# Gather buffers, edge weights and slot tiles in a four-layer graph network: which buffers a gather waits for

## The chip, the cores and the metric

The kernel runs on one core of one Trainium2 chip. The metric is the device time of one execution in microseconds. Three executions took 8439.02, 8420.99 and 8424.09 us, so the median is 8424.09 us. The profiled execution is a separate one and took longer than these; its numbers stand below.

## The reference

The input is a graph with 12,500 nodes of 128 features and 212,500 edges that are sorted by destination. Four layers follow each other; each one normalizes the node rows, gathers the row of every edge's source node, and adds a message into the row of the edge's destination node. Cut to what matters:

```python
h = relu(layernorm(x))                       # ahead of every layer
# layer 0: attention with 4 heads of 32
Wh = (h @ W.T).reshape(N, 4, 32)
attn = leaky_relu((concat([Wh[src], Wh[dst]], -1) * a).sum(-1), 0.2) + edge_attr_16 @ W_e.T
alpha = segment_softmax(attn, dst)
x = x + layernorm(gelu(segment_sum(alpha[..., None] * Wh[src], dst)))
# layer 1: weighted sum
x = x + gelu(gelu(segment_sum(h[src] * edge_weight1, dst)) @ W.T + b)
# layer 2: tensor product of h[src] with 9 edge features, a 32x32 mix for each path, sum over dst
x = x + segment_sum(tensor_product(h[src], edge_attr_9), dst)
# layer 3: mean over the neighbours, then a batch norm over the nodes
mean = segment_sum(h[src], dst) / maximum(segment_sum(1, dst), 1)
x = x + batchnorm(mean @ W_l.T + b_l + h @ W_r.T)
```

## The kernel before

**Tiles.** An edge group is 1024 edges, 8 slots of 128 (T = 8); there are NG = 208 groups. Because edges are sorted, the destinations of one group fall into a window of 128 nodes, so the sum over destinations is a matrix product of the 128 gathered rows with a one-hot matrix (`oh`), added up over the 8 slots in PSUM and then added into the accumulator `acc` (128 features by nodes) at the window's start.

**Gathers.** Each of the 8 slots of a group is one indirect DMA, issued from the POOL queue (`gather`, L621 to L624): 128 indices, 128 rows. Layers 0, 1 and 2 gather all 208 groups, that is 1664 gathers each. The 8 gathers of a group fill one tile `X`, and the pool of such tiles has a fixed depth: `bufs=LAG + 3`, which is 10, in layer 0 (L778), 4 in layer 1 (L1083), 4 in layer 2 (L1102), 3 in layer 3 (L1317). A gather of group g waits until the readers of the group that held the tile before are done. Gathers share eight completion semaphores, so each one waits also for the gather eight before it to have landed.

**Order.** In the edge loops the order on each engine is written out by hand (`manual_schedule`): per iteration of g, layer 1 gathers group g, builds its one-hot on DVE (L1085), adds group g-2 into `acc` (L1088) and multiplies group g-1 on PE (L1093). Layer 2 runs, per iteration, the ACT scaling A of group g (L1123), the mixer product of group g+1 (L1110 to L1113), the one-hot (L629), the add of group g-3 (L1158), the DVE products of group g (L1130 to L1142), the PE products of group g-1 (L1148) with their copy `R` on ACT (L1150, L1151), and the product `po` of group g-2 (L1155). Layer 0 trails its gathers by LAG = 7 groups, because the softmax weights of a group (`weights`, L800 to L846) are worked out four groups at a time; `spread_out` (L848) multiplies messages (L855, L860) and counts the edges of each node with a second product (L862), which DVE adds into `cnt` (L867).

**Between layers.** The first gather of a layer waits for all rows of the table that the node stage of the layer before stores (`htab`, `tab3`), so POOL idles there.

**Layer 3.** Only the first G0 = 138 groups, whose destinations lie in the first 64 blocks of 128 nodes (W0_ = 64), go through gathers. The sources of the other 34 windows (NW) are sorted in layer 1 (`Slots`, L905 to L1065) into slot tiles, 26 for each window, 884 in all. A slot tile (`tabled`, L1189 to L1287) takes four products `px` from a table in SBUF (L1256), a copy to `xb` on ACT (L1267) and one product `pw` (L1240); before each run of seven tiles, `fetch` and `prepare` load and build their one-hots (L1245, L1246). In the loop (L1314 to L1357), from g = 10 to 137, the tiles due in an iteration run first (L1336 to L1342) and then the eight products of group g-1 (L1348). One step of a node chunk (`node3`, four blocks of 128 nodes, 25 chunks) follows in each iteration, one chunk at a time (L1355 to L1357); a chunk has eight steps and divides by the counts: a load of `cnt16` (L521), a product that spreads it (L524), a maximum (L527), a reciprocal (L528) and a multiplication (L530). At the end `closing` applies the batch norm.

**Edge weights.** `eww` (L195, 6.5 KB in each partition) is loaded at the start (L307) and stays to the end. Layer 1 uses it, and so does a general path (from L1364) that runs only for graphs the windows don't fit.

Of the kernel before, what the change touches and what calls it, by code (L numbers as in the profile page):

```python
# [24 lines left out]
P = 128  # L25
T = 8
# [64 lines left out]
def gnn_kernel(ctx: ExitStack, tc, x, src, dst, ef16, ef9, ew, W0, We0, a0, lns, lnb, W1, b1,  # L91
# [18 lines left out]
    OT = OV // 4  # L110
    assert NS % P == 0
# [83 lines left out]
    eww = cst.tile([P, NG, T], F, name="eww")  # L195
# [3 lines left out]
    rough = cst.tile([P, 1], I, name="rough")  # L199
    begin = cst.tile([P, NW], I, name="begin")  # L200
# [9 lines left out]
    with tc.tile_pool(name="ed", bufs=1) as ep:  # L210
# [42 lines left out]
        vec.tensor_scalar(bi3, base, float(W0_ * P + 2 * W), None, op0=ALU.min)  # L253
# [37 lines left out]
        vec.scalar_tensor_tensor(worst, many, float(W), worst, op0=ALU.mult, op1=ALU.max)  # L291
        vec.tensor_scalar(many, red[:, 0, G0 - GM - 1 : G0 - GM], W0_ * P - 0.5, None, op0=ALU.is_gt)
# [14 lines left out]
    load_edges(eww, ew.rearrange("e o -> (e o)"), 0, NG, 0.0, 1)  # L307
# [98 lines left out]
    cnt16 = dram.tile([1, AW], B16, name="cnt16")  # L406
# [40 lines left out]
    def node0(sp, pp, k):  # L447
        b0, nb = k * NBK, min(NBK, NB - k * NBK)
        xv = sp.tile([P, nb, D], F, name="xv")
        load_rows(xv, x, b0, nb)  # L450
        pa = pp.tile([P, nb, P], F, name="pa")
        for j in range(nb):
            pe.transpose(pa[:, j, :], acc[:, (b0 + j) * P : (b0 + j + 1) * P], ident)
        yield
        vec.memset(acc[:, cols(k)], 0.0)
        o = sp.tile([P, nb, D], F, name="o")
        act.activation(o, pa, AF.Gelu)
        yield
        for n in norm(sp, o, nb, None):
            if n is None:  # L460
                yield
            else:
                o = n
        vec.tensor_tensor(o, o, lns_b[:, None, :].to_broadcast([P, nb, D]), ALU.mult)
        vec.tensor_tensor(o, o, lnb_b[:, None, :].to_broadcast([P, nb, D]), ALU.add)
        vec.tensor_tensor(xv, xv, o, ALU.add)
        yield from keep(sp, 0, k, xv)
# [48 lines left out]
    def node3(sp, pp, k, tabS, stats):  # L516

        b0, nb = k * NBK, min(NBK, NB - k * NBK)
        n = min(NBK * P, N - b0 * P)
        cn = sp.tile([1, nb * P], B16, name="cn")  # L520
        nc.sync.dma_start(cn, cnt16[:, cols(k)])  # L521
        yield
        pc = pp.tile([P, nb * P], F, name="pct")
        pe.matmul(pc, ones16, cn, start=True, stop=True)  # L524
        yield
        am = sp.tile([P, nb * P], F, name="am")
        vec.tensor_scalar(am, pc, 1.0, None, op0=ALU.max)  # L527
        vec.reciprocal(am, am)  # L528
        yield
        vec.tensor_tensor(am, acc[:, cols(k)], am, ALU.mult)  # L530
        pt = pp.tile([P, nb, P], F, name="pct")
        for j in range(nb):
            for i in range(3):
                pe.matmul(pt[:, j, :], tabS[:, b0 + j, i * P : (i + 1) * P], ident16, start=i == 0, stop=i == 2)
        yield
        hT = sp.tile([P, nb * P], F, name="hT")
        act.copy(hT, pt.rearrange("p j n -> p (j n)"))
        yield
        po = pp.tile([P, nb * P], F, name="pn")
        pe.matmul(po, WlT, am, start=True, stop=False)  # L540
        pe.matmul(po, WrT, hT, start=False, stop=True)  # L541
        yield
        act.activation(acc[:, cols(k)], po, AF.Identity, bias=bl_c)
        yield
        vec.bn_stats(stats[:, k, :], acc[:, b0 * P : b0 * P + n])
# [79 lines left out]

    def one_hot(sp, r, wgt=None, dt=F):
        s = sp.tile([P, T, W], dt, name="oh")
        if wgt is None:
            vec.tensor_tensor(s, iop[:, None, :].to_broadcast([P, T, W]), r[:, :, None].to_broadcast([P, T, W]),  # L629
                              ALU.is_equal)  # L630
        else:
            for t in range(T):
                vec.tensor_scalar(s[:, t, :], io, r[:, t : t + 1], wgt[:, t : t + 1], op0=ALU.is_equal, op1=ALU.mult)  # L633
        return s

    class Window:
# [7 lines left out]
        def load(self, b):  # L644
            ins, vals = nc.values_load_multi_w_load_instructions(b, engines=(self.engine,), min_val=0, max_val=AW - W)
            if len(self.ends) >= 2 and not self.ordered:
                for i in ins:
                    tc.add_manual_dep(i.ins, self.ends[-2].ins.name, NOSYNC, reason="registers")
            return vals[0]
# [4 lines left out]
    def sweep(xp, stream, window):  # L654
# [83 lines left out]

    H1 = H + 1
    vec.memset(acc, 0.0)  # L740
    with (tc.tile_pool(name="e0", bufs=2) as sp, tc.tile_pool(name="e0p", bufs=2, space=PSUM) as pp,
# [18 lines left out]
        cnt = sp.tile([1, AW], B16, name="cnt", bufs=1)  # L760
# [14 lines left out]
        def logits(g):  # L775

            e, rb, sdw = loads.pop(g)
            X = xs[g] = sp.tile([P, T, P + H], F, name="X", bufs=LAG + 3)  # L778
# [21 lines left out]
        def weights(i):  # L800
# [3 lines left out]
            d = sp.tile([P, L + 1], I, name="d")  # L804
            nc.sync.dma_start(d[:n], windows(dpad, c - HALO - 1, n, K, L + 1))
            lt = sp.tile([P, L, H], F, name="lt")
# [41 lines left out]
        def spread_out(g):  # L848

            X, ev = xs.pop(g), alphas.pop(g)  # L850
            S = sp.tile([P, T, W], F, name="oh")
            vec.tensor_tensor(S, iop[:, None, :].to_broadcast([P, T, W]),
                              rel[:, g, :, None].to_broadcast([P, T, W]), ALU.is_equal)
            msg = sp.tile([P, T, P], F, name="msg")
            vec.tensor_tensor(msg.rearrange("p t (h d) -> p t h d", h=H),  # L855
                              X[:, :, :P].rearrange("p t (h d) -> p t h d", h=H),
                              ev[:, :, :, None].to_broadcast([P, T, H, HD]), ALU.mult)
            pag = sums[g] = pp.tile([P, 2, W], F, name="pag", bufs=1)
            for t in range(T):
                pe.matmul(pag[:, 0, :], msg[:, t, :], S[:, t, :], start=t == 0, stop=t == T - 1)  # L860
            for t in range(T):
                pe.matmul(pag[:1, 1, :], ones[:, :1], S[:, t, :], start=t == 0, stop=t == T - 1)  # L862

        def add_up(g):
            win = ds(areg.load(bi[0:1, g : g + 1]), W)
            p = sums.pop(g)
            vec.tensor_tensor(cnt[:, win], cnt[:, win], p[:1, 1, :], ALU.add)  # L867
# [199 lines left out]
    kept = ctx.enter_context(tc.tile_pool(name="kept", bufs=1))  # L1067
    relc = kept.tile([P, NW, NT], F, name="relc")
    oversrc = kept.tile([SL, NW], I, name="oversrc")


    with (tc.tile_pool(name="e1", bufs=3) as sp, tc.tile_pool(name="e1p", bufs=2, space=PSUM) as pp,
# [6 lines left out]
        with tc.manual_schedule():  # L1079
            g = -1  # L1080
            while nodes.step(g := g + 1) or g < NG + 2:
                if g < NG:
                    X[g] = sp.tile([P, T, P], F, name="X", bufs=4)  # L1083
                    gather(X[g], htab[0], si[:, g, :])
# [4 lines left out]
                if 0 <= g - 1 < NG:  # L1089
                    p = pags[g - 1] = pp.tile([P, W], F, name="pag")  # L1090
                    s, r = S.pop(g - 1), X.pop(g - 1)
                    for t in range(T):
                        pe.matmul(p, r[:, t, :], s[:, t, :], start=t == 0, stop=t == T - 1)  # L1093
                slots.step(1 + g % 2)
            slots.close()


    def layer2(sp, pp):
        feats = feature_stream(ef9f, 9, 4, "ef", sp)

        def rows2(idx):
            X = sp.tile([P, T, P], F, name="X", bufs=4)  # L1102
# [59 lines left out]
    with (tc.tile_pool(name="e2", bufs=3) as sp, tc.tile_pool(name="e2p", bufs=2, space=PSUM) as pp,  # L1162
          tc.tile_pool(name="n2", bufs=2) as ns, tc.tile_pool(name="n2p", bufs=1, space=PSUM) as np_):
        rows2, mix, _, window2 = layer2(sp, pp)
# [24 lines left out]
    def tabled(sp, pp, xb, tabS, pm, stats, make):  # L1189
# [23 lines left out]
        def last(i):  # L1213

            xo = sp.tile([P, 3 * P], B16, name="xo")
            pool.indirect_dma_start(out=xo[:SL, :], out_offset=None, in_=tab3[:, :],
# [3 lines left out]
        def finish(i, pw):  # L1220
            s = sp.tile([P, P], F, name="s3", bufs=1)
            vec.tensor_reduce(s, pw.rearrange("p (k f) -> p f k", k=3), AX.X, ALU.add)
# [19 lines left out]
        for i in range(NW):  # L1242
            pw = None
            for jp in range(0, NT, PT):
                fetch(k + 2)  # L1245
                prepare(k + 1)  # L1246
                a, b = ready.pop(k)
                for jj in range(pieces[k][2]):
# [9 lines left out]
                    if j == OT:  # L1258
                        x = xo
                        act.copy(x[SL : 2 * SL, :], px[SL : 2 * SL, :])  # L1260
                        act.copy(x[2 * SL :, :], px[2 * SL :, :])
                        if i + 1 < NW:
                            xo = last(i + 1)
                    else:
                        x = xb[n_x % len(xb)]
                        n_x += 1
                        act.copy(x, px)  # L1267
                    if len(pend) == 2:
                        scatter()
                    if pw is None:  # L1270
                        while pend and pend[0][3]:
                            scatter()
                        pw = pp.tile([P, 3 * P], F, name="pw", bufs=1)
                    pend.append((x, b[:, jj, :], pw, j))
                    ends = [e for e in ends if next(e, "end") != "end"]
# [13 lines left out]
    with tc.tile_pool(name="l3", bufs=1) as lp:  # L1289
        stats = lp.tile([P, NK, 6], F, name="stats")  # L1290
        with (tc.tile_pool(name="t3", bufs=1) as tp, tc.tile_pool(name="e3", bufs=2) as sp,
# [3 lines left out]
            xb = [tp.tile([P, 3 * P], B16, name=f"xb{i}") for i in range(4)]  # L1295
# [7 lines left out]
            with tc.manual_schedule():  # L1303
# [10 lines left out]
                while g < G0 + 8 or alive or going or waiting:  # L1314
                    g += 1
                    if g < G0:
                        X[g] = sp.tile([P, T, 3 * P], B16, name="X", bufs=3)  # L1317
                        gather(X[g], tab3, si[:, g, :])
# [17 lines left out]
                    if alive and g >= first:  # L1336
                        goal = total if g >= last_ else total * (g - first + 1) // (last_ - first + 1)
                        while alive and (count < goal or goal == total):
                            alive = next(windows3, "end") != "end"
                            count += 1  # L1340
                            if g >= last_ and count % 8 == 0:
                                break  # L1342
                    h = g - 1
                    if 0 <= h < G0:
                        p = sums[h] = pp.tile([P, 3 * P], F, name="pg")
                        s, r = S.pop(h), X.pop(h)
                        for t in range(T):
                            pe.matmul(p, s[:, t, :], r[:, t, :], start=t == 0, stop=t == T - 1)  # L1348
# [16 lines left out]
    with tc.If(coarse > W - 1):  # L1365
        with tc.tile_pool(name="dm", bufs=1) as dp:
# [7 lines left out]
            with tc.tile_pool(name="e0s", bufs=1) as sp, tc.tile_pool(name="e0sp", bufs=1, space=PSUM) as pp:  # L1374
# [96 lines left out]
                sweep(sp, stream0, window0)  # L1471
# [16 lines left out]
        def plain(table, weighted, cnt=None):  # L1488
            with tc.tile_pool(name="es", bufs=1) as sp, tc.tile_pool(name="esp", bufs=1, space=PSUM) as pp:
# [20 lines left out]
                sweep(sp, stream, window)  # L1510
# [5 lines left out]
        with tc.tile_pool(name="es2", bufs=1) as sp, tc.tile_pool(name="es2p", bufs=1, space=PSUM) as pp:  # L1516
            sweep(sp, *layer2(sp, pp)[2:])
        stages(lambda sp, pp, k: node2(sp, pp, k, False), "s2")
        with tc.tile_pool(name="s3", bufs=1) as lp:
# [5 lines left out]
            with tc.tile_pool(name="sc", bufs=1) as sp, tc.tile_pool(name="scp", bufs=1, space=PSUM) as pp:  # L1525
                closing(sp, pp, stats)

# [22 lines left out]
```

## Time and profile before

| what | value |
|---|---|
| median of 3 executions | 8424.09 us |
| profiled execution, device time | 10645.62 us |
| its span | 10643.7 us |
| PE, DVE, ACT, POOL busy in the span | 5167.9, 5258.0, 1588.9, 5829.3 us |
| gathers from `X` lines | 3328 + 2768 = 6096 |
| mean granted TensorE clock | 0.697 of full |
| DMA | 681.72 MB, mean 64 GB/s |

PE, DVE, ACT and POOL are the engines for matrix products, vector work, activations and gathers. "Busy" counts instructions in execution; of a gather, [...]the rows land later. "Idle before, releaser" tells how long an engine waited ahead of an instruction and what ended the wait; "issue" means nothing that the profile shows, "remote" an event whose sender it does not name. The profiled execution is 2221.5 us longer than the median, so its waits must not be read as the median's.

### The profile page before, as it was taken

What the parts mean: (1) busy time and instruction counts of PE and PEld (TensorE: products, weight loads), DVE (VectorE), ACT (ScalarE), POOL (GpSimd) and SP (SyncE); (2) the same over time, 40 slices, a digit from 0 to 9 for tenths busy, and PEclk for the clock granted to TensorE, in tenths of its full rate; (3) what the DMA queues carried; (4) which work ended last, traced back from release to release, by engine and by line L of the source; (5) the groups of instructions that cost most, each with busy time, mean ns of one, the idle gap of its engine ahead of it and who ended that gap; (6) DMA issues with size and microseconds to landing.
All of it is one profiled execution on the core that took longest, in us unless ns stands there. A gap on an engine that the chain in (4) does not pass through costs nothing. (4 is left out here: it accounts for less than half of the span.)

```text
span 10643.7 us, 98234 instructions
## 1 busy us (share of the span) xinstructions
PE 5167.9 (49%) x32393; PEld 4059.5 (38%) x32394; DVE 5258.0 (49%) x10427; ACT 1588.9 (15%) x4187; POOL 5829.3 (55%) x6154
## 2 busy tenths in 40 slices
PE   3355555555533333333235555555655545545545
PEld 2244444444433333332235555555555522212212
DVE  5355555555555455553236666666666632323223
ACT  1000100100000000000012222222222212222222
POOL 0655555555536666666654554555555555555552
PEclk9877676667766666666567777777777766766666
DMA  5333333333312222222211111111111132222222
GB/s 85 77 86 83 82 87 85 82 84 84 85 39 53 55 55 55 53 55 56 55 49 42 47 45 44 49 45 46 47 46 45 45 104 72 75 72 73 72 71 77
DMA packets 718359, 681.72 MB, mean 64 GB/s; under 512 B 341854, under 2 KB 593270, under 8 KB 717815
## 3 DMA queue, kind: packets, MB, share of 16 engines
q0 software_dynamic: 213824, 440.32, 16.9%
q1 hardware_dynamic: 504012, 235.02, 8.8%
q8 instruction: 256, 4.19, 0.2%
q14 instruction: 267, 2.19, 0.1%
HBM read 612.44 MB, written 63.25 MB: 63 GB/s over the span
## 5 line engine op out<-in xcount | busy, mean ns | idle before, releaser
L623 POOL DMA_INDIRECT X<-htab,si x3328 | 3157.8, 949 | 2354.5 <-issue 1934.1
L623 POOL DMA_INDIRECT X<-tab,si x2768 | 2637.4, 953 | 2011.5 <-issue 802.5
L1093 PE MATMUL pag<-oh,X 128*128 128x128 f32 x3328 | 696.3, 374 | 765.8 <-DVE acc L1088 344.6
L1093 PEld LDWEIGHTS pag<-oh,X 128*128 128x128 f32 x3328 | 621.2, 277 | 890.8 <-issue 406.3
L860 PE MATMUL pag<-oh,msg 128*128 128x128 f32 x3328 | 715.0, 402 | 412.4 <-DVE msg L855 294.5
L860 PEld LDWEIGHTS pag<-oh,msg 128*128 128x128 f32 x3328 | 659.1, 303 | 433.1 <-DVE msg L855 307.8
L1256 PE MATMUL px<-tabS,oha 128*32 128x384 bf16 x3502 | 365.3, 407 | 771.8 <-issue 403.8
L1113 PE MATMUL py<-mixer,eT 72*128 72x120 f32 x416 | 143.6, 442 | 1177.0 <-ACT eT L1112 955.2
L629 DVE TENSOR_TENSOR oh<-iop,rel 128x1024 f32<-128x1024 f32 (+1 forms) x338 | 410.7, 1215 | 569.0 <-remote 242.8
L1148 PE MATMUL pag<-oh,A 128*128 128x128 f32 x3328 | 681.3, 391 | 0.0
L1148 PEld LDWEIGHTS pag<-oh,A 128*128 128x128 f32 x3328 | 664.5, 305 | 0.4 <-ACT R L1151 0.4
L1267 ACT CAST xb<-px 128x384 bf16<-128x384 f32 x850 | 398.8, 479 | 1446.7 <-remote 945.2
L1158 DVE TENSOR_TENSOR acc<-acc,po 128x128 f32 x208 | 59.8, 288 | 1047.8 <-remote 863.6
L867 DVE TENSOR_TENSOR cnt<-cnt,pag 1x128 f32 x208 | 57.6, 277 | 1038.4 <-remote 578.3
L1113 PEld LDWEIGHTS py<-mixer,eT 72*128 72x128 f32 x416 | 90.9, 272 | 1245.6 <-ACT eT L1112 1002.6
L1123 ACT ACTIVATE A<-X,ef 128x128 f32<-128x128 f32 x1664 | 510.0, 393 | 12.3 <-DMA X<-htab,si 12.3
L862 PE MATMUL pag<-oh,ones 128*1 128x128 f32 x3328 | 504.4, 316 | 11.5 <-issue 11.5
L785 PE MATMUL pt<-WeB,eT 128*128 128x32 f32 x416 | 109.0, 350 | 823.2 <-ACT eT L783 541.8
L1256 PEld LDWEIGHTS <-oha 128*32 128x32 bf16 x3502 | 115.5, 96 | 1018.9 <-issue 1006.6
L1148 PE MATMUL pag<-oh,B 128*128 128x128 f32 x3328 | 468.1, 301 | 0.0
L1148 PEld LDWEIGHTS pag<-oh,B 128*128 128x128 f32 x3328 | 462.3, 222 | 0.0
L633 DVE TENSOR_SCALAR oh<-io,rel,eww 128x128 f32<-128x128 f32 x1664 | 447.7, 357 | 11.1 <-issue 11.0
(377 smaller groups left out, 8877.2 us busy)
## 6 DMA issues: line engine op xcount, KB each, us to landing
rb<-rel SPq DMA_DIRECT2D x208, 256.0 KB
X<-htab,si POOLq DMA_INDIRECT x3328
X<-tab,si POOLq DMA_INDIRECT x2768
lob<-lo SPq DMA_DIRECT2D x102, 224.0 KB
xtab<-xv SPq DMA_DIRECT2D x72, 256.0 KB
xv<-xtab SPq DMA_DIRECT2D x72, 256.0 KB
ef<-in_edge_attr_dram SPq DMA_DIRECT2D x51, 256.0 KB
htab<-t SPq DMA_DIRECT2D x48, 256.0 KB
```

Source lines behind the costliest of these rows:

```text
L623: pool.indirect_dma_start(out=t[:, s, :], out_offset=None, in_=table[:, :], in_offset=bass.IndirectOffsetOnAxis(ap=idx[:, s : s + 1], axis=0))
L629: vec.tensor_tensor(s, iop[:, None, :].to_broadcast([P, T, W]), r[:, :, None].to_broadcast([P, T, W]), ALU.is_equal)
L633: vec.tensor_scalar(s[:, t, :], io, r[:, t : t + 1], wgt[:, t : t + 1], op0=ALU.is_equal, op1=ALU.mult)
L785: pe.matmul(pew, eT, WeB, start=True, stop=True)
L860: pe.matmul(pag[:, 0, :], msg[:, t, :], S[:, t, :], start=t == 0, stop=t == T - 1)
L862: pe.matmul(pag[:1, 1, :], ones[:, :1], S[:, t, :], start=t == 0, stop=t == T - 1)
L1093: pe.matmul(p, r[:, t, :], s[:, t, :], start=t == 0, stop=t == T - 1)
L1113: pe.matmul(py[:, 1, : T * NY], eT, mixer, start=True, stop=True)
L1123: act.activation(A[:, t, :], X[:, t, :], AF.Copy, scale=e[:, t, 0:1])
L1148: pe.matmul(pag[: TPK[c] * HD, c, :], lhs, S[:, t, :], start=t == 0, stop=t == T - 1)
L1256: pe.matmul(px[q * SL : (q + 1) * SL, :], a[:, jj * P + q * SL : jj * P + (q + 1) * SL], tabS[:, blk, :], start=True, stop=True)
L1267: act.copy(x, px)
```

## The change

What it does, part by part:

1. **Layer 1**: a group's rows are eight tiles of their own (`gather_apart`), 96 in all; each is free when its one product is done.
2. **Layer 3**: the same, with 36 row tiles.
3. **Layer 2**: 11 group tiles where there were 4. **Layer 0**: 12 where there were 10; some small tiles of layer 0 (`d`, `lt`, `o`) go from two buffers to one.
4. **Edge weights**: `eww` lives in a pool that opens just ahead of layer 0 and closes after layer 1. Its load moves from the start to that place; the general path loads its own copy. `relc` and `oversrc` move to the constant pool.
5. **Counts**: layer 0 counts edges only for the first 138 groups. For the last 34 windows the count comes out of the slot tiles: `xb` and `xo` get one more column of ones, `pw` has 385 columns, and `finish` divides by the last one. Node chunks with b0 of 64 and more skip the load, the spreading product, the maximum, the reciprocal and the multiplication, and have five steps.
6. **Slot tiles interleaved**: the tiles due in an iteration of layer 3 are spread between the eight products of the group; `fetch` and `prepare` come after the third tile of a run and not ahead of it.

```diff
-    eww = cst.tile([P, NG, T], F, name="eww")
-    load_edges(eww, ew.rearrange("e o -> (e o)"), 0, NG, 0.0, 1)
...
+    early = ExitStack()
+    eww = early.enter_context(tc.tile_pool(name="ewp", bufs=1)).tile([P, NG, T], F, name="eww")
+    load_edges(eww, ew.rearrange("e o -> (e o)"), 0, NG, 0.0, 1)
     H1 = H + 1
     vec.memset(acc, 0.0)
...
+    def gather_apart(sp, table, idx, bufs):
+        ts = []
+        for s in range(T):
+            ts.append(sp.tile([P, table.shape[1]], table.dtype, name="X", bufs=bufs))
+            pool.indirect_dma_start(out=ts[-1], out_offset=None, in_=table[:, :],
+                                    in_offset=bass.IndirectOffsetOnAxis(ap=idx[:, s : s + 1], axis=0))
+        return ts
...
-            X = xs[g] = sp.tile([P, T, P + H], F, name="X", bufs=LAG + 3)
+            X = xs[g] = sp.tile([P, T, P + H], F, name="X", bufs=LAG + 5)
...
-            for t in range(T):
+            for t in range(T if g < G0 else 0):
                 pe.matmul(pag[:1, 1, :], ones[:, :1], S[:, t, :], start=t == 0, stop=t == T - 1)
...
-                    X[g] = sp.tile([P, T, P], F, name="X", bufs=4)
-                    gather(X[g], htab[0], si[:, g, :])
+                    X[g] = gather_apart(sp, htab[0], si[:, g, :], 12 * T)
...
-                        pe.matmul(p, r[:, t, :], s[:, t, :], start=t == 0, stop=t == T - 1)
+                        pe.matmul(p, r[t], s[:, t, :], start=t == 0, stop=t == T - 1)
...
-        rows2, mix, _, window2 = layer2(sp, pp)
+        rows2, mix, _, window2 = layer2(sp, pp, 11)
...
+        am = acc[:, cols(k)]
+        if b0 < W0_:
...
...
-            vec.tensor_reduce(s, pw.rearrange("p (k f) -> p f k", k=3), AX.X, ALU.add)
+            vec.tensor_reduce(s, pw[:, : 3 * P].rearrange("p (k f) -> p f k", k=3), AX.X, ALU.add)
+            r = sp.tile([P, 1], F, name="r3", bufs=1)
+            vec.tensor_scalar(r, pw[:, 3 * P :], 1.0, None, op0=ALU.max)
+            vec.reciprocal(r, r)
+            vec.tensor_scalar(s, s, r, None, op0=ALU.mult)
...
-                        X[g] = sp.tile([P, T, 3 * P], B16, name="X", bufs=3)
-                        gather(X[g], tab3, si[:, g, :])
+                        X[g] = gather_apart(sp, tab3, si[:, g, :], 36)
...
-                    if alive and g >= first:
-                        goal = total if g >= last_ else total * (g - first + 1) // (last_ - first + 1)
...
-                        for t in range(T):
-                            pe.matmul(p, s[:, t, :], r[:, t, :], start=t == 0, stop=t == T - 1)
+                    for t in range(T):
+                        if 0 <= h < G0:
+                            pe.matmul(p, s[:, t, :], r[t], start=t == 0, stop=t == T - 1)
+                        goal = total * (T * (g - first) + t + 1) // (T * (last_ - first + 1))
+                        while alive and count < min(goal, total + T):
+                            alive = next(windows3, "end") != "end"
+                            count += 1
```

## The prediction, made before the changed kernel ran

> **What bounds the kernel now.** I read the page first, then the busy times by stage, then timelines inside the stages.
>
> ```profile
> span 10643.7 us, 98234 instructions
> ...
> POOL 0655555555536666666654554555555555555552
> PEclk9877676667766666666567777777777766766666
> ...
> L623 POOL DMA_INDIRECT X<-htab,si x3328 | 3157.8, 949 | 2354.5 <-issue 1934.1
> L623 POOL DMA_INDIRECT X<-tab,si x2768 | 2637.4, 953 | 2011.5 <-issue 802.5
> ```
>
> No engine is full: POOL runs at five or six tenths from the first gather to the last. The two gather rows are what orders everything: 6096 gathers, 5795 us busy, and 4366 us of idle ahead of them.
>
> ```profile
> 6018.78 0.94 POOL L623 DMA_INDIRECT X<-htab,si  x1 [0.30 <-issue]
> 6029.61 0.95 POOL L623 DMA_INDIRECT X<-htab,si  x1 [9.89 <-issue]
> 6030.87 0.94 POOL L623 DMA_INDIRECT X<-htab,si  x1 [0.30 <-issue]
> 6032.11 0.95 POOL L623 DMA_INDIRECT X<-htab,si  x1 [0.30 <-issue]
> ```
>
> The timeline of POOL in layer 2 splits that idle time. 0.30 us belongs to every gather, so gathers come at best every 1.247 us, 9.98 us a group. The 9.89 us is a wait for a buffer: it ends 0.74 us after DVE's last reader of an old `X` tile (6028.87 us).
>
> ```profile
> 245.70:2937.10 2691.40, 1382.83 (x8680) 1094.69 (x8680) 1389.62 (x3191) 240.18 (x476) 1591.57 (x1665) 0.71 0.35 84
> 3052.30:5427.20 2374.90, 813.68 (x4858) 730.80 (x4858) 1066.30 (x2919) 116.20 (x161) 1585.12 (x1665) 0.60 0.21 54
> 5452.50:8508.90 3056.40, 1748.31 (x11664) 1669.24 (x11664) 1917.16 (x2450) 660.97 (x2334) 1572.85 (x1666) 0.74 0.17 46
> 8569.90:10489.70 1919.80, 960.81 (x5861) 374.90 (x5862) 548.13 (x806) 442.31 (x938) 1075.50 (x1138) 0.68 0.30 78
> ```
>
> These are layers 0 to 3, first gather to last (start:end, length, then busy time of PE, weight loads, DVE, ACT, POOL, PE clock, DMA). Outside them lie the start (245.7 us), three gaps between layers (115.2, 25.3 and 61.0 us) and the end (154.0 us).
>
> **The floor under the median.** 6096 gathers at 1.247 us and 34 of L1216 at 1.17 us (0.87 + 0.30) make 7641 us; with the start, gaps and end 601 us, 8242 us. The span is 10643.7 us, so it holds 2401 us of POOL waits. The median, 8424, holds 182 if its gathers have the same pace: the profiled execution shows mostly waits that the median can't have. They look like late signals of PE: in layer 2 the products of `pag` are recorded as ended at 6043.0 us, and ACT's copy, which waits for them, starts at 6049.7. So I take durations and orders from the trace and the stall from the median. That recording lengthens PE's signals but not POOL's 1.247 us is an assumption: the pace is the same to 0.01 us in all four layers.
>
> **Start.** The `eww` load goes. Its 32-byte packets, about 26,500, fill the DMA engines from about 38 to 52 us in the trace's packets, and the loads of `seq` behind them land at 56.8 us, ahead of DVE's checks, the weights and the node table. Cost removed: 14 us at most; I take 13, as short loads stand beside it. The load is now issued ahead of layer 0's first feature and `rb` loads on SP's queue, so layer 0's compute begins some 14 us later. POOL does not wait for that: it has two groups (20 us) more of buffers. If the cover is gone, 13 us come back. **-13 us.**
>
> **Layer 0's end.** After the last gather the remaining groups run one after another:
>
> ```profile
> 3004.85 1.91 PE L862 MATMUL pag<-oh,ones 128*1 128x128 f32 x16
> 3006.80 0.28 DVE L867 TENSOR_TENSOR cnt<-cnt,pag 1x128 f32 x1 [3.98 <-PE pag L862]
> ```
>
> DVE's add waits for the counting product, and the next group's one-hot follows the add. From group 138 on both are left out: 1.91 + 0.2 us in each group, where ten messages (L855) lie between 2941 and 3029 us. Six come after the last softmax weights and count fully, four partly: 6 x 2.1 and half of 4 x 2.1. **-15 us** (bounds -21 and -8). Earlier in the layer it lies beside the gathers and is worth nothing.
>
> **The end.** Node chunks take one step per iteration, eight steps each. Counting along the loops (L1314 to L1357), at g = 137 chunk 21 has just started, and nine follow: 10, 11, 22, 12, 13, 23, 14, 24, 15. In the trace they stand in a row from 10502 to 10599 us, each 10.05 us:
>
> ```profile
> 10522.37 0.60 PE L524 MATMUL pct<-cn,ones 1*128 1x512 bf16 x1
> 10523.81 0.67 DVE L527 TENSOR_SCALAR am<-pct 128x512 f32<-128x512 f32 x1
> 10524.52 3.35 DVE L528 RECIPROCAL am<-am 128x512 f32<-128x512 f32 x1
> 10527.90 0.69 DVE L530 TENSOR_TENSOR am<-acc,am 128x512 f32<-128x512 f32 x1
> 10532.43 0.60 PE L524 MATMUL pct<-cn,ones 1*128 1x512 bf16 x1
> ```
>
> Chunks 16 to 24 now have five steps, so the backlog shrinks: at g = 137 chunk 11 is under way, and 22, 12, 13, 23, 14, 24, 15 follow. A short chunk leaves out L524 to L530; PE is late next: 1.44 (L534) + 2.05 + 1.92 (L540, L541) = 5.4 us. Then 4 x 10.05 + 2 x 5.4 + 3.5 (chunk 24 has two blocks) + 3 for the rest of 11 = 57.5 us stands for 96.7. **-38 us** (bounds -30 and -43). The price is in `finish`: three small DVE operations for each of 34 windows, about 0.15 us each like L423, and one column in 385; DVE is busy 548 of 1920 us there, so nothing.
>
> **Added waits on POOL.** With tiles of their own, 2636 gathers in layers 1 and 3 wait for PE as well as for the gather eight before; before, one gather in eight did. A second wait is an instruction of its own on POOL, and behind it all later gathers stand.
>
> ```profile
> L623 POOLq EVENT_SEMAPHORE  x214: 17/17/43, 3051.0 to 5429.4; - x107
> ```
>
> In layer 1 the longest of these took 43 ns, and at least half of the gathers behind one started 0.31 us after the end of their predecessor, the usual gap. With 96 tiles the products waited for are twelve groups old. Cost nothing; if the queue can't run ahead, 0.70 us passes from a released wait to the gather (6040.29 to 6040.99 us in layer 2) in place of 0.30, that is 0.40 us for each.
>
> **Deeper buffers.** They can win only from the 182 us. Below: nothing; above: all. In layer 1, DVE (1066 us of 2375) and PE are far from full; three groups of slack suffice unless PE is late. Layer 2 decides. There a loop runs PE, ACT, PE: from the end of the C products at 6032.48 us, `R`, eight A copies, `eT` and the mixer product take 3.6 us until the next products start, and these are 48 instructions of 0.11 us, 5.3 us at full clock. The period is 5.3 / clock + 3.6: 8.9 us at full, 14.2 at half, 9.98 at a clock of 0.83. The row says 0.74, which makes 10.8 us, 0.8 above the gathers' pace in 208 groups, 170 us: nearly the whole 182, and no buffer changes it. [...]the clock should stay up, the loop should be shorter than the gathers and only swings be left, which eleven tiles absorb; then all 182 go. The row's 0.74 was taken with late signals, which lengthen the idle time, so I stand between: half, **-75 us** of the 150 or so that lie in the layers. Layer 3's tiles spread between products belong to this: PE is busy 961 of 1920 us, and no longer holds eight products, and so the row tiles, behind seven slot tiles. Moving `fetch` and `prepare` by three tiles leaves four tiles, over 2 us, until they are needed: nothing.
>
> **Sum.** 8424 - 13 - 15 - 38 = 8358; less 75 is 8283, say **8280 us**. In the profiled execution the same edits take 66 us and the buffers much more, as its waits are larger: a span of about 9,700 us.
>
> **Rivals.**
> - *The loop in layer 2 bounds* (20%): buffers give nothing, **8358 us**. For it: clock 0.74. Against: late signals in the same rows.
> - *POOL never waits* (20%): 8358 - 182 = **8176 us**, less if gathers are quicker when nothing is recorded: 2% of their pace is 150 us. For it: eleven tiles hold 110 us of rows. Against: layer 2's DVE has 9.2 us of work in a group (1917 / 208), close to 9.98.
> - *The waits on POOL cost* (5%): 0.40 us x 2636 = 1054 us, **9330 us**, slower; from 360 gathers on (one in seven) it eats the other gains. For it: an instruction more before each gather. Against: 43 ns at most.
> - *Placing moves nothing or the removed steps come back elsewhere* (5%): about 8424, a little on either side.
>
> **How the numbers follow.** The forecast has 50%, and these four the rest. A measurement here tells 0.2%, about 17 us, from no change. Faster takes the forecast and the first two, 90%; 3% for the same and 7% for slower come from the last two. The range reaches from 8120, past the floor by a part of the quicker gathers, to 8400, past the first rival by the bounds of the small terms.
>
> **What would show it.** First gather near 233 us; gap after layer 0 near 100 us; from the last gather to the end near 116; layer 1 near 2,080 us with gathers 1.247 us apart; in layer 2 POOL running eleven groups ahead and then waiting, if the loop bounds, or never waiting, if not. Gathers at 1.6 us in layer 1 would make the third rival true. A gather pace other than 1.247 us in unrecorded runs would make the floor wrong, and no view shows that.

## The result: 0.7% less, and where it came from

The changed kernel took 8372.41 us (median of 4, 8361.61 to 8374.21), the kernel before, in the same rounds, 8424.94 us (8420.99 to 8439.02): a ratio of 0.9932, 95% interval 0.9915 to 0.9949. In a second set of rounds it was 8358.68 against 8429.85 us, ratio 0.9918 (0.9904 to 0.9931). So the change is worth 53 to 71 us by these medians, and not the 144 us of the forecast. 8358, the number of the first rival, lies closest.

The page of the changed kernel, whose recording (8370.70 us) is close to its median:

```profile
span 8368.4 us, 98356 instructions
...
POOL 0677777777747777777776777777666637777773
PEclk7687778765555555555555888888888876787777
...
L629 POOL DMA_INDIRECT X<-htab,si x1664 | 1573.5, 946 | 621.7 <-issue 570.6
L637 POOL DMA_INDIRECT X<-htab,si x1664 | 1583.6, 952 | 560.7 <-issue 255.1
L629 POOL DMA_INDIRECT X<-tab,si x1664 | 1595.0, 959 | 507.4 <-issue 484.3
```

POOL is busy seven tenths of nearly every slice. The rows are layers 2, 1 and 0: a gather takes what it took before, 0.95 us, and layer 2 has some 60 to 110 us more idle time ahead of its 1664 gathers than the other two. A hole of POOL (the 3) comes behind layer 2.

The recording of the kernel before that stands above the prediction was a disturbed execution, 26% longer than its median. It was recorded once more (experiment 1), with a span of 8436.5 us, and that one is compared here. The busy times by stage, first the changed kernel's layer 2, the gap behind it, layer 3 and the end (start:end, length, busy PE, weight loads, DVE, ACT, POOL, then PE clock, DMA share, GB/s):

```profile
4531.50:6726.60 2195.10, 1645.56 (x11378) 1590.12 (x11379) 1871.57 (x2388) 646.91 (x2285) 1573.70 (x1665) 0.83 0.24 63
6726.60:6845.00 118.40, 80.12 (x577) 77.11 (x576) 90.54 (x145) 30.41 (x103) 0.20 (x1) 0.80 0.20 60
6845.00:8269.00 1424.00, 1019.14 (x5942) 280.69 (x5943) 560.19 (x940) 456.77 (x952) 1077.57 (x1138) 0.75 0.39 101
8269.00:8368.40 99.40, 50.83 (x229) 29.11 (x227) 43.24 (x54) 28.28 (x42) 0.20 (x1) 0.71 0.47 132
```

The same four stretches of the kernel before:

```profile
4547.20:6811.90 2264.70, 1699.83 (x11680) 1643.31 (x11681) 1922.07 (x2458) 663.68 (x2343) 1573.36 (x1666) 0.82 0.22 62
6811.90:6867.10 55.20, 36.88 (x276) 35.20 (x275) 38.80 (x71) 13.98 (x45) 0.19 (x1) 0.81 0.11 33
6867.10:8293.50 1426.40, 1040.93 (x5910) 350.76 (x5911) 548.26 (x812) 452.84 (x948) 1079.97 (x1138) 0.74 0.38 104
8293.50:8436.50 143.00, 74.35 (x271) 38.60 (x269) 69.74 (x73) 30.71 (x46) 0.20 (x1) 0.57 0.33 91
```

Layer 2's gathers end 70 us sooner with eleven tiles, and the gap behind them is 63 us longer. POOL runs ahead, and then stands at the first gather of layer 3 until the computation has come after it. Only the end is really shorter. Taken together, in us:

| stretch | before, experiment 1 | changed | difference |
|---|---|---|---|
| start to the first gather | 243.5 | 230.9 | -12.6 |
| layer 0, first to last gather | 2100.7 | 2102.0 | +1.3 |
| gap after layer 0 | 94.2 | 91.7 | -2.5 |
| layer 1 and its gap | 2108.9 | 2107.0 | -1.9 |
| layer 2 and its gap | 2319.9 | 2313.5 | -6.4 |
| layer 3 | 1426.3 | 1424.0 | -2.3 |
| last gather to the end | 143.1 | 99.4 | -43.7 |

The sum is -68 us. The start and the end, two of the small edits, make 56 of it. The stall that buffers were to remove is in one place: gathers further apart than 1.26 us lose 185.6 us in layer 2 of the kernel before, and 21.7, 13.0 and 6.1 us in layers 0, 1 and 3 (what each distance has above 1.26 us, added up).

### The profile page after: what moved, and what is told of

The parts are those of the page before. It is cut to its first block, busy times and chain, and to the rows that moved or that the text cites. A ratio compares the mean times of both kernels' runs of the same rounds, so it can differ in the third digit from the quotient of the medians.

```text
span 8368.4 us, 98356 instructions
## 1 busy us (share of the span) xinstructions
PE 5398.6 (65%) x31264; PEld 3935.6 (47%) x31265; DVE 5222.0 (62%) x10472; ACT 1589.8 (19%) x4187; POOL 5834.5 (70%) x6154
## 4 chain that ended last, share of the span: by engine, by line
## 5 line engine op out<-in xcount | busy, mean ns | idle before, releaser
L1110 PE MATMUL pag<-oh,X 128*128 128x128 f32 x3328 | 1239.8, 483 | 746.8 <-DMA X<-htab,si 709.4
L1110 PEld LDWEIGHTS pag<-oh,X 128*128 128x128 f32 x3328 | 808.4, 306 | 1162.5 <-DMA X<-htab,si 1066.6
L637 POOL DMA_INDIRECT X<-tab,si x1104 | 1048.1, 949 | 415.4 <-issue 99.6
L878 PE MATMUL pag<-oh,msg 128*128 128x128 f32 x3328 | 663.4, 380 | 626.6 <-DVE msg L873 626.6
L878 PEld LDWEIGHTS pag<-oh,msg 128*128 128x128 f32 x3328 | 613.2, 285 | 647.1 <-DVE msg L873 647.1
L1368 PE MATMUL pg<-X,oh 128*128 128x384 bf16 x1104 | 441.3, 415 | 389.2 <-DMA X<-tab,si 227.6
L1167 PEld LDWEIGHTS pag<-oh,A 128*128 128x128 f32 x3328 | 645.1, 297 | 0.4 <-ACT R L1170 0.4
L1105 DVE TENSOR_TENSOR acc<-acc,pag 128x128 f32 x208 | 59.8, 288 | 800.0 <-PE pag L1110 758.5
L1158 DVE TENSOR_TENSOR term<-X,py 128x768 f32<-128x768 f32 x416 | 395.3, 950 | 7.1
L1167 PE MATMUL pag<-oh,C 128*96 128x128 f32 x3328 | 397.3, 273 | 0.0
L1169 ACT COPY R<-pag 128x256 f32<-128x256 f32 x208 | 77.4, 372 | 1572.2 <-PE pag L1167 1572.2
```

The source lines that it names most:

```text
L637: pool.indirect_dma_start(out=ts[-1], out_offset=None, in_=table[:, :], in_offset=bass.IndirectOffsetOnAxis(ap=idx[:, s : s + 1], axis=0))
L1110: pe.matmul(p, r[t], s[:, t, :], start=t == 0, stop=t == T - 1)
L1158: vec.tensor_tensor(o, x1[:, :, i : i + 1, :].to_broadcast(v3), Y[:, :, 3 + 3 * i : 6 + 3 * i, None].to_broadcast(v3), ALU.mult)
L1167: pe.matmul(pag[: TPK[c] * HD, c, :], lhs, S[:, t, :], start=t == 0, stop=t == T - 1)
L1368: pe.matmul(p, s[:, t, :], r[t], start=t == 0, stop=t == T - 1)
```

## The experiments

Times are medians of five executions unless it is said otherwise. They were taken in four sets, each with the kernel before in the same rounds, and a ratio is always to that one: 8417.75 us for experiment 1, the two edits of 2 and the first kernel of 3; 8429.85 us for the changed kernel again, the other two of 3 and the first of 5; 8429.38 us for 4; 8428.76 us for the second of 5 and both of 6. The theory: layer 2 is bound by its loop PE, ACT, PE; so buffers can't help. The rival: buffers were worth about half of the stall.

### 1. The kernel before, recorded again

> The kernel before, recorded once more, for a profile near its median. Theory (layer 2 is bound by its own loop PE, ACT, PE): its span is near 8420 us; the time from layer 2's first gather to layer 3's first gather is 2310 us, as in the changed kernel (2313.5), but spent differently: POOL waits inside the layer with four tiles, and the gap before layer 3 is near 60 us where the changed kernel has 118. The start is 245 us, the gap after layer 0 is 115, the end from the last gather is near 150, against 231, 92 and 99. Rival (deeper buffers did win about half of the stall, and the small edits less than thought): the stretch of layer 2 is 60 us or more longer than 2313, and start, gap and end differ less from the changed kernel's.

It took 8438.44 us (one execution). From layer 2's first gather to layer 3's it is 2319.9 us, with 55 us of gap, as the theory had it. Start and end came out as expected, but the gap after layer 0 is 94.2 us and not 115: that number belonged to the disturbed recording.

### 2. Buffers put back

Layer 2 alone, then all four layers, in the first set; the changed kernel ran again in the second. First:

```diff
-        rows2, mix, _, window2 = layer2(sp, pp, 11)
+        rows2, mix, _, window2 = layer2(sp, pp)
```

> The changed kernel with 4 group tiles in layer 2 where it has 11, all else kept. Theory (the loop bounds layer 2): the same time as the changed kernel, 8372 us within 15; the last gather of layer 2 comes later and the gap before layer 3 shrinks from 118 to about 60 us. Rival (the tiles are worth half of the stall or more): 50 us or more slower, 8420 or above.

8347.91 us, ratio 0.9916 (0.9902 to 0.9929).

```diff
-            X = xs[g] = sp.tile([P, T, P + H], F, name="X", bufs=LAG + 5)
+            X = xs[g] = sp.tile([P, T, P + H], F, name="X", bufs=LAG + 3)
...
-                    X[g] = gather_apart(sp, htab[0], si[:, g, :], 12 * T)
+                    X[g] = sp.tile([P, T, P], F, name="X", bufs=4)
+                    gather(X[g], htab[0], si[:, g, :])
...
-                        X[g] = gather_apart(sp, tab3, si[:, g, :], 36)
+                        X[g] = sp.tile([P, T, 3 * P], B16, name="X", bufs=3)
+                        gather(X[g], tab3, si[:, g, :])
...
```

> The changed kernel with the buffers of all four layers as before (10, 4, 4 and 3 group tiles), with the counts, the place of the edge weights and the interleaved slot tiles as changed. Theory (buffers are worth next to nothing, since layer 2 is bound by its loop and the others have slack): 8375 us, within 20. The forecast's step (75 us for the buffers): 8447 us.

8345.17 us, ratio 0.9916 (0.9903 to 0.993).

> The changed kernel as it is, timed on the same chip and in the same rounds as the three others of this set. Theory (its buffers are worth nothing while layer 2's loop bounds): about 8365 us, within 20 of what the kernel with all four depths put back took (8345.17).

8358.68 us, ratio 0.9918 (0.9904 to 0.9931). Three ratios that agree to 0.0002 (the first measurement's 0.9932 was a little higher): four kinds of deeper buffers are together worth nothing that these rounds can tell (each interval is 0.0027 wide, about 23 us). The forecast's 8447 us is refuted. With four tiles in layer 2, the stretch and its gap are these:

```profile
4527.80:6778.20 2250.40, 1688.21 (x11681) 1631.56 (x11682) 1921.15 (x2458) 663.84 (x2343) 1573.07 (x1666) 0.83 0.22 62
6778.20:6830.40 52.20, 33.82 (x275) 32.13 (x273) 38.55 (x75) 13.99 (x45) 0.24 (x2) 0.86 0.12 35
```

2302.6 us together, where eleven tiles took 2313.5 and 2303.2; with all depths put back it was 2290.0. Depth decides whether POOL waits inside the layer or behind it.

### 3. The loop opened

```diff
-                if g + 1 < NG:
-                    mixed[g + 1] = mix(g + 1)
                 step(g)
                 step(g - 3)
                 step(g)
                 step(g - 1)
+                if g + 1 < NG:
+                    mixed[g + 1] = mix(g + 1)
                 step(g - 2)
```

> The changed kernel with one move in layer 2: the mixer product of group g+1, with its transpose and its copy on ACT, comes after the PE products and the copy of group g-1, not before them, so that PE's products no longer wait for eight ACT scalings of another group. Theory (the loop PE, ACT, PE bounds layer 2): the loop sheds about 2.5 us a group, gathers bound the layer at 9.98 us, and the stretch from layer 2's first gather to layer 3's goes from 2313 to about 2150 us: 8210 us, 160 less. Rival (DVE's 9.0 us of work in a group and the node steps bound the layer): under 40 us less.

8166.55 us, ratio 0.97 (0.9687 to 0.9713), 43 us better than expected. Layer 2 with its gap:

```profile
4529.50:6608.10 2078.60, 1565.43 (x11871) 1477.35 (x11872) 1923.20 (x2482) 757.87 (x2374) 1571.94 (x1665) 0.91 0.24 67
6608.10:6640.70 32.60, 10.58 (x85) 9.40 (x83) 18.25 (x52) 5.23 (x14) 0.23 (x2) 0.78 0.60 183
```

2078.6 us are 1664 gathers 1.249 us apart: in this layer POOL hardly waits any more (14 gathers come later than 1.26 us after the one before). DVE does the same 1920 us of work, so it did not bound the layer. Does this need the deep buffers?

> The mixer product after the products of the group before, as in the 8166.55 us kernel, but with the buffers of all layers as before (10, 4, 4, 3 group tiles). Theory (with the loop out of the way gathers bound every layer at 1.249 us, and four tiles cover the swings): 8170 us, within 15. Rival (deep buffers begin to pay once the loop no longer bounds: a node step or a slow pass of PE stops the gathers): 30 us or more slower, 8200 or above.

8165.78 us, ratio 0.969 (0.9677 to 0.9703): no. And on the kernel before, with the one move and nothing of the change:

> The kernel before with the one move in layer 2 alone: the mixer product of group g+1 after the products of group g-1; four tiles, counts, edge weights and slot tiles as before. Theory: the same 205 us as on the changed kernel, 8417 - 205 = 8212 us. Rival (it needs the eleven tiles): 8270 or above.

8225.39 us, ratio 0.9761 (0.9748 to 0.9775). The move alone is worth three times the whole change, and the change's other parts are worth 59 us on top of it (8225 to 8166), what they were worth without it.

### 4. Why the loop was so long: PE's clock

Opening the loop shortens the chain and also lets PE wait less, so it can't tell whether the waits or the clock made it long. Here is PE in layer 2 of the changed kernel:

```profile
5801.16 0.78 PE L1132 MATMUL py<-mixer,eT 72*128 72x120 f32 x2 [2.39 <-ACT eT L1131]
5801.74 3.15 PE L1167 MATMUL pag<-oh,A 128*128 128x128 f32 x16
5804.73 1.95 PE L1167 MATMUL pag<-oh,B 128*128 128x128 f32 x16
...
5811.59 0.48 PE L1132 MATMUL py<-mixer,eT 72*128 72x120 f32 x2 [1.95 <-ACT eT L1131]
5811.91 1.96 PE L1167 MATMUL pag<-oh,A 128*128 128x128 f32 x16
...
5822.81 0.78 PE L1132 MATMUL py<-mixer,eT 72*128 72x120 f32 x2 [4.64 <-ACT eT L1131]
5823.39 3.63 PE L1167 MATMUL pag<-oh,A 128*128 128x128 f32 x16
```

In brackets is the wait for `eT`. After waits of 2.39 and 4.64 us the 16 products of `A` take 3.15 and 3.63 us, after 1.95 us they take 1.96. Over the layer, worked out from the trace: the 48 products of a group take 5.49 us at best and 7.00 us in the mean, and of 159 groups whose longest wait before them was 2.3 to 3.0 us, nine in ten took over 6.2.

The trace also holds the clock that was granted to PE. Over the 48 products of each of these three groups, in the changed kernel (columns as before; the first busy time is PE's, the number behind the POOL column is the granted clock):

```profile
5801.74:5808.42 6.68, 6.68 (x51) 6.68 (x51) 6.01 (x7) 0.00 (x0) 4.54 (x6) 0.81 0.19 48
5811.91:5817.40 5.49, 5.49 (x52) 5.49 (x51) 5.35 (x6) 0.00 (x0) 3.40 (x5) 1.00 0.23 61
5823.39:5831.14 7.75, 7.75 (x51) 7.75 (x51) 7.58 (x12) 0.00 (x0) 3.77 (x4) 0.69 0.17 42
```

PE is at work all the time, and a group takes 6.68 us at 0.81 and 7.75 at 0.69, where 5.49 stand at 1.00. Worked out over layer 2 of this trace: of 207 groups (all but the first), the 178 that took over 6.2 us had a mean clock of 0.65 to 0.82 over their products, and the other 29 had 1.00 throughout. The wait just before a group doesn't tell its clock alone: of the 25 groups without a wait of 2 us since the group before, 13 took over 6.2 us too.

The last experiment on this layer keeps the order and gives PE idle work in that wait:

```diff
-        def mix(g):
+        def mix(g, fill=False):
...
             act.copy(eT, py[: T * 9, 0, :])
+            if fill:
+                d = pp.tile([P, 3, W], F, name="pag", bufs=1)
+                for t in range(8):
+                    pe.matmul(d[:1, 0, :], ones[:, :1], ident, start=t == 0, stop=t == 7)
...
-                    mixed[g + 1] = mix(g + 1)
+                    mixed[g + 1] = mix(g + 1, True)
```

> The changed kernel, order of layer 2 as it is (mixer product ahead of the products of the group before), with eight more products of ones and the identity, about 1.9 us, put in PE's queue where it waits for eT; nobody reads their result. Theory (after a wait of 2.3 to 3.0 us PE's clock is halved, so that the 48 products of a group take 7.0 us for 5.5, and this makes the loop longer than the gathers): the products take 5.5 us, the loop 9.4 us for 10.9, the stretch from layer 2's first gather to layer 3's goes from 2303 or 2313 to between 2110 and 2170 us, the time to 8160 to 8220 us. Rival (the loop is long because of ACT's copies and the node stages on its way, the clock is a consequence): 8359 us within 20, or slower by what the added products delay the mixer product.

8170.34 us, ratio 0.9696 (0.9682 to 0.971). The theory's lower end, and the rival is out: work of which nobody reads the result saves some 190 us, and the mean clock of the layer, first gather to last, is 0.96 for 0.83. PE in that kernel:

```profile
5792.49 0.48 PE L1136 MATMUL py<-mixer,eT 72*128 72x120 f32 x2 [1.61 <-ACT eT L1131]
5792.81 1.96 PE L1171 MATMUL pag<-oh,A 128*128 128x128 f32 x16
5794.60 1.95 PE L1171 MATMUL pag<-oh,B 128*128 128x128 f32 x16
5796.39 1.91 PE L1171 MATMUL pag<-oh,C 128*96 128x128 f32 x16
...
5799.01 1.91 PE L1135 MATMUL pag<-ident,ones 128*1 128x128 f32 x16
5804.83 0.48 PE L1136 MATMUL py<-mixer,eT 72*128 72x120 f32 x2 [3.91 <-ACT eT L1131]
5805.15 3.37 PE L1171 MATMUL pag<-oh,A 128*128 128x128 f32 x16
```

L1135 is the idle work. Where 1.61 us of wait are left, the products of `A` take 1.96 us; where a node step holds ACT and 3.91 us are left, they take 3.37. In the mean a group's products take 5.68 us for 7.00, while the time between two groups' products doesn't shrink (4.31 us for 3.93): it is the products that made the loop too long. Layer 2 with its gap takes 2116.5 us.

### 5. The end of layer 0

The forecast's second step, 15 us, came to 2.5. The drain of the last groups, in the kernel before (experiment 1) and then in the changed one:

```profile
2389.06 2.05 PE L860 MATMUL pag<-oh,msg 128*128 128x128 f32 x16 [2.83 <-DVE msg L855]
2391.04 1.91 PE L862 MATMUL pag<-oh,ones 128*1 128x128 f32 x16
2395.77 2.05 PE L860 MATMUL pag<-oh,msg 128*128 128x128 f32 x16 [2.83 <-DVE msg L855]
```

```profile
2375.61 3.78 PE L878 MATMUL pag<-oh,msg 128*128 128x128 f32 x16 [2.64 <-DVE msg L873]
2382.03 3.78 PE L878 MATMUL pag<-oh,msg 128*128 128x128 f32 x16 [2.64 <-DVE msg L873]
```

The counting products are gone, and the message products take 3.78 us in place of 2.05: a group takes 6.42 us where it took 6.71. The granted clock agrees. Here are two groups of the drain in the first recording of the kernel before, where they lie as far apart as in the second, and then two of the changed kernel (columns as above):

```profile
3002.87:3009.59 6.72, 3.89 (x33) 3.12 (x33) 2.73 (x4) 0.00 (x0) 0.00 (x0) 1.00 0.00 0
3009.59:3016.30 6.71, 3.89 (x32) 3.12 (x32) 2.73 (x4) 0.00 (x0) 0.00 (x0) 1.00 0.01 2
```

```profile
2375.61:2382.03 6.42, 3.78 (x16) 3.48 (x17) 2.55 (x3) 0.00 (x0) 0.00 (x0) 0.50 0.00 0
2382.03:2388.46 6.43, 3.79 (x17) 3.49 (x17) 2.55 (x3) 0.00 (x0) 0.00 (x0) 0.50 0.00 0
```

To have the clock back, the first try kept the products where they were:

```diff
-            for t in range(T if g < G0 else 0):
+            for t in range(T):
                 pe.matmul(pag[:1, 1, :], ones[:, :1], S[:, t, :], start=t == 0, stop=t == T - 1)
```

> The changed kernel, but PE still multiplies the ones by the one-hot for the last 70 groups of layer 0; nobody reads the result, and DVE adds counts for the first 138 groups only. Theory (without these products PE is less busy while the last groups of layer 0 drain, its clock is halved there and the message products take 3.78 us for 2.05, which eats the gain of the edit): at full clock a group takes DVE's 2.8 us, 2.05 of PE and little else, about 4.9 us for 6.42, so the gap after layer 0 goes from 91.7 to about 82 us and the time falls by 10. Rival (DVE's add waits for the count product all the same): 6.5 us a group, no gain.

8367.34 us, ratio 0.9932 (0.9919 to 0.9946), a gap of 101.6 us: the rival. The messages took 2.02 us again, but DVE's add still waited for the counting product (L880), which writes to the same tile:

```profile
2381.22 0.29 DVE L889 TENSOR_TENSOR acc<-acc,pag 128x128 f32 x1 [4.04 <-PE pag L880]
```

A group takes 6.59 us; why the gap is even longer than in the kernel before (94.2) isn't shown. The second try puts them behind the add:

```diff
...
             areg.end(vec.tensor_tensor(acc[:, win], acc[:, win], p[:, 0, :], ALU.add))
+            S = hots.pop(g)
+            for t in range(T if g >= G0 else 0):
+                pe.matmul(p[:1, 1, :], ones[:, :1], S[:, t, :], start=t == 0, stop=t == T - 1)
```

> The mixer product late and the changed buffers (8166.55 us), and, for the last 70 groups of layer 0, PE's product of ones and one-hot behind DVE's add of the group, so that nothing waits for it and PE runs while DVE builds the next one-hot and messages; nobody reads its result. Theory (PE's halved clock ate the gain of leaving these products out): the message products take 2.05 us again, a draining group about 5 us for 6.42, the gap after layer 0 goes from 91.6 to about 82 us, and the time to 8157 us. Rival (the clock is halved for another reason, or DVE still waits): a gap of 91 us or more and 8166 us.

8161.79 us, ratio 0.9684 (0.967 to 0.9697), with a gap of 85.5 us: 6 us less, where 10 were expected.

```profile
2365.90 3.57 PE L892 MATMUL pag<-oh,ones 128*1 128x128 f32 x16 [23.50 <-DVE acc L889]
2369.53 2.91 PE L878 MATMUL pag<-oh,msg 128*128 128x128 f32 x16
2372.82 1.91 PE L892 MATMUL pag<-oh,ones 128*1 128x128 f32 x16 [0.38 <-DVE acc L889]
2375.17 2.02 PE L878 MATMUL pag<-oh,msg 128*128 128x128 f32 x16 [0.45 <-DVE msg L873]
2377.57 1.91 PE L892 MATMUL pag<-oh,ones 128*1 128x128 f32 x16 [0.38 <-DVE acc L889]
```

A draining group now takes 4.76 us; in the first one the products still take 3.57 and 2.91 us. The gap shows the gain, the medians (8166.55 in another set) are too close to show it by themselves.

### 6. Two small parts by themselves

Both on the kernel with the opened loop, where executions lie within 6 us of each other. First the edge weights at the start:

```diff
+    eww = cst.tile([P, NG, T], F, name="eww")
...
+    load_edges(eww, ew.rearrange("e o -> (e o)"), 0, NG, 0.0, 1)
     ef16f = ef16.rearrange("e f -> (e f)")
...
-    eww = early.enter_context(tc.tile_pool(name="ewp", bufs=1)).tile([P, NG, T], F, name="eww")
-    load_edges(eww, ew.rearrange("e o -> (e o)"), 0, NG, 0.0, 1)
```

> The kernel of 8165.78 us (mixer product late, all depths as before) with the edge weights loaded at the start and kept to the end, as before. Theory: the first gather comes 13 us later, 243 us for 230, nothing else moves: 8179 us. Rival (the load is hidden at the start, and the earlier first gather comes from somewhere else): 8166 us.

8177.78 us, ratio 0.9703 (0.969 to 0.9717), the first gather at 243.2 us for 229.9: as expected. Then the slot tiles in a row, as in the kernel before:

```diff
-                    for t in range(T):
-                        if 0 <= h < G0:
-                            pe.matmul(p, s[:, t, :], r[t], start=t == 0, stop=t == T - 1)
-                        goal = total * (T * (g - first) + t + 1) // (T * (last_ - first + 1))
...
+                    if alive and g >= first:
+                        goal = total if g >= last_ else total * (g - first + 1) // (last_ - first + 1)
...
```

> The kernel of 8166.55 us (mixer product late) with the slot tiles of an iteration in a row ahead of the eight products, and the one-hots fetched and prepared ahead of a run of seven, as before. Theory (layer 3 is bound by its gathers, PE is busy 1019 of 1424 us): layer 3 2 us longer, the end unchanged at 99 us, 8168 us within 5. Rival (interleaving gave a part of the 44 us by which the end is shorter): the end at 105 us or more, 8173 or above.

8169.58 us, ratio 0.9692 (0.9679 to 0.9705): layer 3's gathers take 1426.9 us for 1425.1, the end 99.3 for 99.1. So interleaving is worth about 2 us, within what two sets of rounds can differ by. The shorter end is neither the interleaving's nor the buffers' (99.6 us with all depths put back): what is left are the steps that the node chunks no longer have, though no run puts the counts back by themselves.

## The prediction, step by step

- **Start, -13.** -12.6 in the comparison of the traces, 12.0 in experiment 6. Right, cover included.
- **Layer 0's end, -15.** -2.5. The step took "1.91 + 0.2 us in each group" off at an unchanged clock (its own sum is 16.8). PE, with less to do between its waits, ran at a clock of 0.50 and gave 1.73 us of the 1.91 back (3.78 for 2.05). Both bounds, -21 and -8, missed it, since in neither did the clock move.
- **The end, -38.** -43.7 (the forecast's own sum, 96.7 less 57.5, is 39.2). Right in mechanism and order of the chunks. A short chunk was priced at 5.4 us with rows at a clock of 0.50; in the changed kernel, shown below, two full chunks are 10.06 us apart, and 12.87 with a short one (8299.69, straight from `acc`) between them, so it costs 2.8 us. Twice 2.6 us makes most of the difference.
- **Added waits on POOL, 0.** Right: gathers in layer 1 stay 1.249 us apart, and layer 1 with its gap takes 2107.0 us for 2108.9. The waits of layer 1, 1568 instructions now, take 17 ns each. The third rival, 9330 us, is out.
- **Price of the counts in layer 3, 0; slot tiles, 0.** Right, within 2 us.
- **Deeper buffers, -75.** This step failed: the buffers gave nothing (experiments 2 and 3), where the prediction gave them half of the stall. Most of the stall was where it looked, in layer 2 (185.6 of 226 us), and its first reading, 10.8 us a group in a loop that no buffer shortens, was the right one (10.98 us in the mean from copy `R` to copy `R` in the second recording). It then set that reading aside. It wrote that "the clock should stay up", so that half of the stall was swings, which tiles absorb; no trace of the kernel before showed that. The runs show otherwise: behind waits of 2.39 us the products of `A` take 3.15 us in the changed kernel and 3.28 in the kernel before, for 1.96 at a clock of 1.00, and a group's products take 7.05 us for 5.49 in the kernel before. The late signals, to which the prediction put down the row's clock of 0.74, did not decide it: the second recording has 0.82, and the loop is as long.

The end of the changed kernel, for the third point of this list:

```profile
8285.08 2.05 PE L546 MATMUL pn<-am,WlT 128*128 128x512 f32 x2 [3.38 <-DVE am L536]
8295.14 2.05 PE L546 MATMUL pn<-am,WlT 128*128 128x512 f32 x2 [3.38 <-DVE am L536]
8299.69 1.10 PE L546 MATMUL pn<-acc,WlT 128*128 128x512 f32 x2
8308.01 2.04 PE L546 MATMUL pn<-am,WlT 128*128 128x512 f32 x2 [3.38 <-DVE am L536]
```

The failed step could have been seen in the profile that stood ahead of it, in the very group from which the prediction took its 3.6 us. Behind a wait of 2.39 us the products of `A` take 3.28 us, and those of `B` 1.95:

```profile
6035.65 0.78 PE L1113 MATMUL py<-mixer,eT 72*128 72x120 f32 x2 [2.39 <-ACT eT L1112]
6036.22 3.28 PE L1148 MATMUL pag<-oh,A 128*128 128x128 f32 x16
6039.34 1.95 PE L1148 MATMUL pag<-oh,B 128*128 128x128 f32 x16
```

The formula, 5.3 / clock + 3.6, was mis-sized in its use of the row: 0.82 gives 10.1 us, 0.9 too few. A mean over a whole stage is not the clock of the products: they take 7.05 us for 5.49, and 3.9 us lie between, as node steps stand on ACT's way. At full clock the formula was good: 8.9 us, against a median of 8.97 where PE was kept busy and no node step stood on ACT's queue.

The second rival's 8176 us, in which POOL never waits, comes true to within 10 us, by the clock or by the order (8170, 8166) and not by tiles; and that the number fits is partly luck. Its 182 us were too few: the 601 us for start, gaps and end were the disturbed recording's, where the second one has 553, so that the same sum makes 230 us of stall (226 in the trace). But some 40 us of such waits are left in these kernels, outside layer 2 for the most part.

What stays open: why the median of the changed kernel differs by 14 us between two sets of rounds (8372.41 and 8358.68) while the opened loop repeats within 6; a loop whose every turn depends on where the clock falls is a likely cause, and only argued. Both remedies in one kernel were not tried, nor idle work with four tiles.

## What to carry to other kernels

Ahead of deeper buffers, measure the time from a stage's first gather to the next stage's first gather, divide it by the groups, and compare it with the gathers' own pace: if the computing loop is longer, buffers only move the wait to the next boundary. Then take the loop apart: an instruction that needs nothing of the loop (here the mixer product of the next group) but stands inside it, on an engine whose order is fixed, belongs behind it. And price a PE step by what the clock does without it: here, taking 1.91 us of products out of a group on which PE waited for nearly half of the time saved 0.29 us, and 1.9 us of idle work in PE's waits saved more (188 us) than the whole change (53 to 71).

## What the hardware showed that was not expected

Groups with the same products took different times, and the granted clock went with it. In layer 2 of the changed kernel the 48 products of a group took 5.49 us at a clock of 1.00, 6.68 at a mean of 0.81 and 7.75 at 0.69. Of 159 groups whose longest wait before them was 2.3 to 3.0 us, nine in ten took over 6.2 us, while in the kernel with idle work 182 groups with under 2 us of wait left took 5.5 us each in the mean.

About the same share of work stood at either clock. In layer 0's drain PE worked for 3.89 us in each 6.72 us at a clock of 1.00 in the first recording of the kernel before, and for 3.78 us in each 6.42 us at 0.50 in the changed kernel. So busy time is not all that the clock goes with; what else, no run here tells.
